# Local attention with queries and keys computed feature-down, their squared lengths taken through DRAM, and the condition set-up moved behind the experts

## The chip, the cores and the metric

The program runs on one core of a Trainium2 chip. The metric is the device time of one execution in microseconds; the time before is the median of three runs. The engines are TensorE (PE), VectorE (DVE), ScalarE (ACT), GpSimd (POOL) and SyncE (SP); the queue from which an instruction or a transfer is issued is named after its engine.

## The reference, cut to what matters

Four sequences of 512 tokens with 256 features pass five stages: a mixture of 8 experts (two per token), a linear attention with 8 heads, a softmax attention with 16 heads whose result is mixed with a "field" that depends on a condition vector per sequence, and two layers of a local attention with a gated feed-forward. Two places matter here.

The local attention of each layer normalises queries and keys, rotates them, and attends within a window:

```python
q = l2norm(q) * qs                 # per head: 8 heads of 64 features
k = l2norm(k) * ksc
q, k = rotary_xpos(q, k)           # t*cos*scale + rotate_half(t)*sin*scale
...
sim = jnp.einsum('bhwid,bhwjd->bhwij', bq, bk)
attn = jax.nn.softmax(sim, axis=-1)
```

The length that `l2norm` divides by belongs to a token and a head. Rotation mixes feature d with feature d+32 of the same head and keeps token and head.

The field is a small chain on the conditions alone, four rows for the four sequences:

```python
fp = _layernorm(jax.nn.relu(consciousness_state @ We1.T + be1) @ We2.T + be2, ln_g, ln_b)
fa = jax.nn.softmax(jnp.einsum('be,se->bs', fp, pe), axis=-1)
```

## The kernel before

The work is one stream of stages: routing and experts, linear attention, softmax attention with conditions, then the local layers. A framework puts waits between instructions and orders each engine's queue by its own model of times; where the program says `PE.in_order()`, PE's queue keeps the order in which the lines are written. All matrices are float32; a matmul leaves two records in the trace.

**Experts (from about L1480).** The chosen tokens of each expert are gathered (POOL's queue), pass three matrices, and are scattered to `ys` in DRAM (POOL's queue). 22 slots run always; two more (`rare`) stand in an `If` on a value read from the chip. The condition set-up `conditions` (L230 to L274: `csb`, `hdT`, a layer norm over four rows to `fp`, two small transposes, the product `pfs` with the position table, a softmax over 512 positions to `fa`, four transposes to `faT`) is called at the last of the 22 slots, ahead of its first layer. Then come three matmuls without use (`busy(3)`), the `If`, six more (`busy(6)`), and the seam: `results(0)` loads `ys` back as `g` (SP's and ACT's queues), `weighted` combines it to `ymoe` (L1530, L1531), and the linear attention starts with transposes of `ymoe`. What `conditions` makes is first used in the softmax attention.

**Local layers (`local_stream`, L563 to L880).** Each sequence ("batch") of a layer has a front, an attention in four steps c (two heads each), and a tail. Order in the loop `for k in range(4 * B + 1)`: scores of step c, first half; fill; values of step c-1; fill; scores of step c, second half; fill. The fill comes from `beside(b)`: the front of batch b+1, the tail of batch b-1, and for the last batch the feed-forward. `spend(n)` takes n pieces of it; before, 2 at each of the three places in batches 0 to 2, and 1 in batch 3. `run(fill)` takes what is left at the start of the next batch. Ahead of the loop, `lead` runs the whole front of batch 0 and two pieces of batch 1's front; for the second layer `lead` is woven with the rest of the first layer's feed-forward, one piece to one.

A front before (L590 to L649) has 22 pieces. It transposes the batch to `yT` (2 pieces), then per token tile and for queries and keys projects with tokens down (`pdq`: 128 tokens x 512 features), takes the squares on ACT (L614), sums them per head on DVE (`ss`, L615), multiplies by the tables from PSUM on DVE (L617, L621) and adds on POOL (`qr`, L624): 8 pieces. Lengths become reciprocals (L628 to L630). The values tiles `v` are 4 pieces. Then `qr` of the queries is scaled (L639) and both are transposed to features down, four transposes and one ACT copy at a time (`pqt`, L642 to L646), 8 pieces. The keys' reciprocal length goes in as the per-partition scale of the exponential (L666, two per tile since the scale differs by key tile). `qT`/`kT` share their memory slots (two each) with `uB`/`uA` of the feed-forward.

Denominators take a trip: `pz` is copied to `z`, written to DRAM (`sums`), read as 128 x 16 (`rden`), inverted, written (`rows`), read back spread over partitions (`zb`), and multiplied into `oT` (L698 to L708), all on SP's queue.

## Time and profile before

| | us |
|---|---|
| three runs | 1388.95, 1391.64, 1391.56 |
| median | 1391.56 |
| profiled execution | 1386.44 |
| its span (first to last instruction) | 1384.7 |
| PE busy in the span | 1335.9 |

| stretch of the span, us | what runs | PE busy, us |
|---|---|---|
| 0 to 310 | routing, experts | 81.7, 100.0, 99.8 in the first three hundreds |
| 310 to 335 | last expert, seam | see the lines that follow |
| 335 to 460 | linear attention | 46.3 of 400 to 450 |
| 460 to 720 | softmax attention | 38 to 49 of each 40 to 50 |
| 720 to 1385 | local layers | 50 of each 50 until 1350, 29.2 of the last 34.7 |

The profile gives for each group of equal instructions a line: line of the program, engine, operation, output<-inputs with partitions x elements, count, then busy time and mean duration in ns, then the engine's idle time just ahead of them and what ended it. In a timeline a line is: start, length, engine, line, operation, count, and in brackets the idle time before it with what released it. Where several instructions are merged the length reaches from the first start to the last end. Matmul records overlap their neighbours at the ends; what a group costs PE is read from its start to the next group's start.

### The profile page before, as it was taken

Reading aid. Unit: us, or ns where it says so; the run is one execution under the profiler, and the core shown is the slowest. Engines: PE = TensorE matmul, PEld = TensorE weight load, DVE = VectorE, ACT = ScalarE, POOL = GpSimd, SP = SyncE. Lnnn points to the kernel's source line nnn. Section 1 sums busy time; section 2 is a strip of 40 time slices with the busy share of each in tenths; the row PEclk is TensorE's granted clock in tenths of the full one; section 3 lists DMA queues with packets and bytes.
Section 4 is the critical chain, followed back from the end, with each engine's and each line's share of the span. In section 5 each row is a group of like instructions: output and inputs, shape, how many; then the busy total and the mean of one; then the engine's idle time right before and its main releaser. Section 6 shows DMA issues by size and latency. Waiting matters only on the chain.

```text
span 1384.7 us, 19465 instructions
## 1 busy us (share of the span) xinstructions
PE 1335.9 (96%) x7632; PEld 827.5 (60%) x7632; DVE 653.3 (47%) x1295; ACT 587.7 (42%) x997; POOL 232.8 (17%) x223
## 2 busy tenths in 40 slices
PE   5999999998999999999999999999999999999998
PEld 4788888874566633333334555656555566556654
DVE  6222212224777643332227687654362777854421
ACT  4111111125555355454655756662223667474111
POOL 1325322211000011010104232100020322310110
PEclk7999999999999999999999999999999999999999
DMA  4577667633000000000210001210001010011000
GB/s 143 209 261 271 226 218 250 208 121 126 1 1 1 1 1 1 1 1 1 88 53 21 17 25 32 78 40 24 23 1 42 24 33 25 17 40 41 22 24 25
DMA packets 43085, 94.74 MB, mean 68 GB/s; under 512 B 9568, under 2 KB 25064, under 8 KB 40168
## 3 DMA queue, kind: packets, MB, share of 16 engines
q1 hardware_dynamic: 37560, 81.81, 17.8%
q0 software_dynamic: 3792, 10.24, 2.2%
q10 hardware_dynamic: 1632, 1.34, 0.3%
q8 instruction: 63, 1.03, 0.3%
q14 instruction: 38, 0.31, 0.1%
HBM read 84.08 MB, written 7.21 MB: 66 GB/s over the span
## 4 chain that ended last, share of the span: by engine, by line
PE 89%; DVE 5%; ACT 2%; DMA 2%; issue 1%; SPq 0%; DVEq 0%; POOLq 0%; POOL 0%; ACTq 0%
PE ph L78 14%; PE pdq L78 12%; PE pfy L78 6%; PE pug L78 5%; PE pv L78 5%; PE pua L78 5%; PE sc L78 5%; PE po L78 4%; PE pn L78 4%; PE pdy L78 4%; PE pds L78 4%; PE pz L78 2%; PE pqt L82 2%; PE pqk L78 1%; PE pf L78 1%
## 5 line engine op out<-in xcount | busy, mean ns | idle before, releaser
L78 PE MATMUL pdq<-wqkv,yT 128*128 128x512 f32 x384 | 177.1, 602 | 0.0
L416 ACT ACTIVATE cex<-sc 128x1024 f32<-128x1024 f32 x128 | 124.0, 1021 | 96.7 <-PE sc L78 95.9
L78 PE MATMUL ph<-h,w 128*128 128x256 f32 (+1 forms) x704 | 133.4, 347 | 0.5 <-ACT h L1398 0.5
L624 POOL TENSOR_TENSOR qr<-t,t 128x512 f32<-128x512 f32 x64 | 85.9, 1343 | 266.4 <-DVE t L621 221.7
L668 DVE TENSOR_TENSOR p<-p,lmask 128x384 f32<-128x384 f32 (+1 forms) x128 | 92.4, 736 | 68.4 <-ACT p L666 67.2
L78 PEld LDWEIGHTS ph<-h,w 128*128 128x128 f32 x704 | 116.1, 191 | 12.9 <-ACT h L1398 0.7
L78 PEld LDWEIGHTS pdq<-wqkv,yT 128*128 128x128 f32 x384 | 69.6, 190 | 78.1 <-issue 72.8
L1398 ACT ACTIVATE h<-ph,w 128x256 f32<-128x256 f32 (+1 forms) x88 | 35.4, 438 | 182.7 <-PE ph L78 130.1
L1400 DVE TENSOR_SCALAR h<-ph,w 128x256 f32<-128x256 f32 (+1 forms) x88 | 36.1, 438 | 162.4 <-PE ph L78 109.2
L666 ACT ACTIVATE p<-pds,ss 128x256 f32<-128x256 f32 (+1 forms) x256 | 96.1, 457 | 39.1 <-PE pds L78 30.6
L78 PE MATMUL pug<-hT,w 128*128 128x512 f32 x160 | 76.8, 602 | 0.0
L78 PE MATMUL sc<-qm,kT 32*128 32x512 f32 x512 | 75.2, 639 | 0.2 <-ACT cex L416 0.2
L78 PE MATMUL pua<-hT,w 128*128 128x512 f32 x160 | 75.2, 592 | 0.0
L614 ACT ACTIVATE sq<-pdq 128x512 f32<-128x512 f32 x64 | 38.3, 598 | 85.2 <-PE pdq L78 49.2
L78 PE MATMUL pv<-cex,v 128*32 128x512 f32 x512 | 69.0, 604 | 2.1 <-DVE xT L290 2.1
L78 PE MATMUL ph<-xbT,w 128*128 128x256 f32 (+1 forms) x352 | 68.5, 347 | 0.5 <-ACT xbT L123 0.5
L387 POOL TENSOR_SCALAR fterm<-vw,faT 128x256 f32<-128x256 f32 x16 | 14.6, 925 | 320.3 <-DVE cr L377 320.3
L78 PE MATMUL po<-w,h 128*128 128x256 f32 x296 | 67.7, 380 | 0.5 <-ACT h L1398 0.5
L78 PE MATMUL pds<-qT,kT 64*128 64x256 f32 (+1 forms) x512 | 65.3, 375 | 0.0
L78 PEld LDWEIGHTS pds<-qT,kT 64*128 64x128 f32 x512 | 43.9, 186 | 32.9 <-issue 25.8
L78 PEld LDWEIGHTS ph<-xbT,w 128*128 128x128 f32 x352 | 58.4, 191 | 7.7 <-issue 0.9
L78 PE MATMUL pdy<-wo,oT 128*128 128x256 f32 x256 | 61.5, 386 | 0.0
(301 smaller groups left out, 2129.9 us busy)
## 6 DMA issues: line engine op xcount, KB each, us to landing
w<-in_moe_w_dram SPq DMA_DIRECT2D x22, 1024.0 KB, 6.3
w<-in_moe_w_dram SPq DMA_DIRECT2D x22, 640.0 KB
w<-in_moe_w_dram SPq DMA_DIRECT2D x22, 516.0 KB, 3.8
zb<-rows SPq DMA_DIRECT2D x32, 256.0 KB, 4.0
g<-ys SPq DMA_DIRECT2D x6, 512.0 KB, 5.1
wqkv<-in_f_wqkv_dram SPq DMA_DIRECT2D x2, 1536.0 KB
w<-in_f_w_dram SPq DMA_DIRECT2D x2, 1408.0 KB, 6.1
out_dram<-yc SPq DMA_DIRECT2D x16, 128.0 KB, 1.8
```

The costliest lines, as they stand in the source:

```text
L78: cls._queue(nc.tensor.matmul(*args, **kw))
L82: cls._queue(nc.tensor.transpose(*args, **kw))
L387: nc.gpsimd.tensor_scalar_mul(fterm[:, t, :], vw, W["faT"][:, t, b : b + 1])
L416: nc.scalar.activation(ex, pss[j], AF.Exp, scale=CHD**-0.5)
L614: nc.scalar.activation(sq, p3, AF.Square)
L624: nc.gpsimd.tensor_tensor(qr_t[:, s], t1, t2, ALU.add)
L666: nc.scalar.activation(p[:, at], pss[r][:, at], AF.Exp, scale=d.ss[:, 2 * u + jj, 1, 2 * c + r : 2 * c + r + 1])
L668: nc.vector.tensor_tensor(p[:, :n], p[:, :n], lmask[:, :n], ALU.mult)
L1398: nc.scalar.activation(dst, src, AF.Relu, bias=bias)
L1400: nc.vector.tensor_scalar(dst, src, bias, 0.0, ALU.add, ALU.max)
```

## The change

1. In the front, queries and keys are projected with features down (`piece`): the weight block is stationary, 512 tokens move. ACT copies the product into `qT`/`kT`; SP copies the partner features (32 partitions apart) to `sw`; ACT squares; DVE multiplies both by the tables (now laid out features down, with the learned scale as a per-partition scalar); POOL adds. No transposes follow.
2. The squares are summed over the 64 features of a head by matmuls with `heads32` (`lengths`); the 16 x 512 sums go to DRAM (ACT's queue), come back as 128 x 64 (POOL's queue), are inverted, go to DRAM again (POOL's queue), come back spread over partitions (`zb`, SP's queue, 8 transfers per front), and scale queries and keys on DVE. The exponential needs no scale and becomes one per tile.
3. A front has 14 pieces. `lead` takes all of the first and 8 of the second; `spend` follows a table; the tail of the batch before comes after 12 pieces. `tab` is loaded once, `b2` with the feed-forward's weights, `zb` has two buffers.
4. `conditions` becomes three parts: the first ahead of the `If`, the second ahead of the seam's last `busy`, the third a filler of the linear attention. Four of the nine matmuls without use go.

```diff
@@ conditions
         nc.vector.tensor_tensor(fp, fp, row("lnb")[:B, :], ALU.add)
+        yield
         pt = tpt("pfpT")
...
         mm(ps[:B, :], [(fpT[:, c, :], W["peT"][:, c, :]) for c in range(2)])
+        fa = cp.tile([B, S], F32, tag="fa", name="fa", bufs=1)
+        nc.vector.tensor_copy(fa, ps[:B, :])
+        yield
...
-        nc.vector.reduce_max(fmx, ps[:B, :], axis=AX.X, negate=True)
+        nc.vector.reduce_max(fmx, fa, axis=AX.X, negate=True)
...
-        nc.scalar.activation(fa, ps[:B, :], AF.Exp, bias=fmx, accum_out=fsum)
+        nc.scalar.activation(fa, fa, AF.Exp, bias=fmx, accum_out=fsum)
@@ local_stream
+        heads32 = dw.tile([128, 32], F32, tag="heads32", name="heads32")
+        nc.gpsimd.memset(heads32, 0.0)
+        for r in range(2):
+            nc.gpsimd.memset(heads32[64 * r : 64 * r + 64, 16 * r : 16 * r + 16], 1.0)
@@ front
+            def piece(s, c):
+                at = s * DIN + c * 128
                 ps = mmt("pdq")
+                mm(ps, [(w.wqkv[:, 0, at : at + 128], yT[:, 0, 1 : S + 1]), (w.wqkv[:, 1, at : at + 128], yT[:, 1, 0:S])])
+                dst = (d.qT, d.kT)[s]
+                nc.scalar.copy(dst[:, c, :], ps)
+                if c % 2 == 0:
+                    return
+                dst = dst[:, c - 1 : c + 1, :]
+                sw = lp.tile([128, 2, S], F32, tag="sw", name="sw", bufs=3)
+                for g in range(4):
+                    nc.sync.dma_start(sw[32 * g : 32 * g + 32], dst[32 * (g ^ 1) : 32 * (g ^ 1) + 32])
+                sqs[s, c // 2] = lp.tile([128, 2, S], F32, tag="sq", name="sq")
+                nc.scalar.activation(sqs[s, c // 2], dst, AF.Square)
+                for i, t in enumerate((sw, dst)):
+                    at = 4 * w.l + 2 * (1 - i) + s
+                    nc.vector.scalar_tensor_tensor(
+                        t, t, qks[:, at : at + 1], tab[:, 2 * s + 1 - i, :].unsqueeze(1).to_broadcast([128, 2, S]),
+                        ALU.mult, ALU.mult)
+                nc.gpsimd.tensor_tensor(dst, dst, sw, ALU.add)
+            def lengths(s):
+                ps = mmt("pl")
+                for c in range(4):
+                    PE.matmul(ps[32 * c : 32 * c + 32, :], heads32, sqs[s, c // 2][:, c % 2, :], start=True, stop=True)
+                z = lp.tile([128, S], F32, tag="z", name="z", bufs=1)
+                nc.scalar.copy(z, ps)
+                nc.scalar.dma_start(sums[s * DH : (s + 1) * DH], z[0:128:16, :])
+            for s in range(2):
+                for c in range(4):
+                    piece(s, c)
+                    if s and c == 1:
+                        lengths(0)
                     yield
...
             for t in range(NT):
...
+                if t == 1:
+                    lengths(1)
+                    rl = lp.tile([128, 2 * DH * S // 128], F32, tag="rl", name="rl", bufs=1)
+                    nc.gpsimd.dma_start(rl, sums.rearrange("h q -> (h q)").rearrange("(p n) -> p n", p=128))
+                    nc.scalar.activation(rl, rl, AF.Sqrt)
+                    nc.vector.tensor_scalar_max(rl, rl, 1e-12)
+                    nc.vector.reciprocal(rl, rl)
+                    rows_ = dr.tile([2 * DH, S], F32, tag="lrows", name="lrows")
+                    nc.gpsimd.dma_start(rows_.rearrange("h q -> (h q)").rearrange("(p n) -> p n", p=128), rl)
+                    for c in (0, 2):
+                        for s, dst in enumerate((d.qT, d.kT)):
+                            zb = lp.tile([128, 2, S], F32, tag="zb", name="zb")
+                            for r in range(2):
+                                nc.sync.dma_start(
+                                    zb[64 * r : 64 * r + 64],
+                                    rows_.rearrange("(s c r) q -> s r c q", r=2, s=2)[s, r, c : c + 2].partition_broadcast(64))
+                            nc.vector.tensor_tensor(dst[:, c : c + 2, :], dst[:, c : c + 2, :], zb, ALU.mult)
                 yield
@@ scores
-                for jj in range(2):
-                    at = slice(jj * 256, min(jj * 256 + 256, n))
-                    nc.scalar.activation(p[:, at], pss[r][:, at], AF.Exp,
-                                         scale=d.ss[:, 2 * u + jj, 1, 2 * c + r : 2 * c + r + 1])
+                nc.scalar.activation(p, pss[r][:, :n], AF.Exp)
@@ values
-            zb = lp.tile([128, 2, S], F32, tag="zb", name="zb", bufs=1)
+            zb = lp.tile([128, 2, S], F32, tag="zb", name="zb")
@@ first_two, beside, the loop
             def lead():
-                for _ in range(20):
-                    next(first)
-                    yield
-                for _ in range(2):
+                yield from first
+                for _ in range(8):
                     next(second)
                     yield
-                yield from first
...
-                    for _ in range(9 if b else 7):
+                    for _ in range(12 if b else 0):
...
+                more = ((2, 3, 2), (2, 2, 1), (1, 1, 1), (1, 1, 1))
+                share = (((1, 1, 1), (1, 0, 0)) + ((0, 0, 0),) * 2, more, more, ((1, 1, 1),) * 4, ((1, 1, 1),))
...
-                    spend(2 if b < B - 1 else 1)
+                    spend(share[b][c][0])
@@ experts, seam
             for j, d in enumerate(often):
-                if j == len(often) - 1:
-                    conditions(cw_, wp)
...
-            busy(3)
+            aside = conditions(cw_, wp)
+            next(aside)
+            busy(1)
             with tc.If(halves > NHALF - NRARE):
...
-            busy(6)
+            busy(3)
+            next(aside)
+            busy(1)
...
-                        fill = (beside(b) if b else chain(rest, beside(0))) if b < B else iter(())
+                        fill = (beside(b) if b else chain(rest, aside, beside(0))) if b < B else iter(())
```

The per-layer scaling of `tab` on DVE, `ss`, `qr` and the transposes of the old front go with it.

## The prediction

> **What bounds the kernel now.** I read the page's busy shares and 40 slices first, then the busy time by stretches, the groups by form, and the timeline at the three places that the change touches.
>
> ```profile
> PE 1335.9 (96%) x7632; PEld 827.5 (60%) x7632; DVE 653.3 (47%) x1295; ACT 587.7 (42%) x997; POOL 232.8 (17%) x223
> ...
> PE   5999999998999999999999999999999999999998
> ```
>
> The stretches (start:end, length, then PE, PEld, DVE, ACT, POOL), two of the local attention:
>
> ```profile
> 850.00:900.00 50.00, 50.00 (x319) 30.31 (x320) 38.26 (x75) 29.14 (x64) 11.08 (x10) 1.00 0.21 65
> ...
> 1150.00:1200.00 50.00, 49.85 (x306) 29.56 (x303) 42.43 (x83) 31.75 (x66) 16.11 (x11) 1.00 0.11 28
> ```
>
> TensorE (PE) works 50 of 50 us, DVE 38 to 42. From 750 to 1350 us PE never rests for as much as 0.5 us, so there a microsecond of PE work is a microsecond of time, and work of the others costs nothing unless PE must wait for it.
>
> **PE work in the local stage.** The projections of queries and keys stay 16 matmuls of 512 columns per front with weights and tokens changing sides (a pair holds PE 1.72 to 1.81 us either way): 0. What goes and what comes:
>
> ```profile
> L78 PE MATMUL pv<-cex,v 128*32 128x512 f32 x512 | 69.0, 604 | 2.1 <-DVE xT L290 2.1
> ...
> L82 PE MATMUL pqt<-ident,qr 128*128 128x128 f32 x256 | 33.9, 277 | 0.8 <-DVE qr L639 0.8
> ```
>
> The 256 transposes (32 in each of 8 fronts) go. Their 33.9 us hold tails that overlap the next group; start to start eight of them hold PE 1.02 us and sixteen 1.89, which is 3.9 to 4.1 us per front, 31.4 in all. `lengths` adds two groups of four 128x32 matmuls of 512 columns per front, 16 groups. `pv` has that very shape: four of them side by side, 64 groups in 69.0 us, 1.08 each; start to start 0.99. I take 16.4 (15.8 to 17.3). Net **-15.0 us**.
>
> DVE and ACT work is covered by PE. DVE per front: before 8 x (0.68 + 0.68 + 0.75) + 4 x 0.68 + 1 = 20.6 us; after 8 products and 4 scalings of 128x1024 at 1.22 (row of L1593) plus 0.8, 15.4. ACT loses half of its 256 exponentials (0.39 start to start). POOL keeps its sum: 4 adds of 128x1024 at 2.44 (row of L751) for 8 at 1.34. The 16 `sw` copies per front pass SP at 0.35 to 0.65 each, some 8 us of a 50 us batch, and are needed only after that front's lengths. If this cover were gone, DVE would have to pass 50 us per batch; it falls. The smaller loads (`tab` once, `qks`, `b2`) lie tens of us ahead of their use: 0.
>
> **The conditions.** In before they stand in front of the last expert.
>
> ```profile
> 304.55 0.28 PE L82 MATMUL pfpT<-ident,fp 4*128 4x4 f32 x2 [1.18 <-DVE fp L254]
> ...
> 305.09 1.88 PE L78 MATMUL pfs<-peT,fpT 128*4 128x512 f32 x4 [0.26 <-DVE fpT L259]
> ...
> 306.90 2.05 PE L78 MATMUL ph<-xbT,w 128*128 128x128 f32 x16
> ...
> 317.23 0.97 POOL L1466 DMA_INDIRECT ys<-ob,goal  x1 [9.14 <-DVE ob L1461]
> ```
>
> They hold PE from 297.40 to 299.65 (2.25 us), from 303.30 to 306.90 (3.60), and about 0.6 more around 309. Without them the last expert, the scatter (317.23) and everything behind come 6.4 us earlier. After, the same work lies in the gap between that scatter and the first `ymoe` (at 325.58; 8 us) and takes the place of four `pbusy`. Price there: the layer norm's ACT step (1.28 table load + 0.29) must end before ACT issues its half of the `g` loads behind the branch, 0 to 1.8 us; the table goes back for the features, 0 to 1.28. I take 1.4: **-5.0 us** (-6.4 to -3.3).
>
> **The added wait.** Lengths used to stay on chip (sqrt, reciprocal, scale, some 3 us). Now they go through DRAM twice, and the first scores of a batch wait for that. The nearest rows are the denominators' trip, on SP's queue:
>
> ```profile
> 782.67 0.63 SPq L698 DMA_DIRECT2D sums<-z  x1
> 784.43 0.34 SPq L699 DMA_DIRECT2D rden<-sums  x1
> 787.50 0.33 SPq L702 DMA_DIRECT2D rows<-rden  x1
> 788.92 1.31 SPq L705 DMA_DIRECT2D zb<-rows  x2
> ```
>
> and DVE's product at its end:
>
> ```profile
> 793.67 1.29 DVE L708 TENSOR_TENSOR oT<-oT,zb 128x512 f32<-128x512 f32 x2 [1.79 <-DMA zb<-rows]
> ```
>
> From the issue of `sums` to the product 11.0 us, hidden because its user comes a batch later. The new trip, from the last `lengths` matmul: ACT copy and issue 1.1; `sums` 1.75; `rl` on POOL's queue; table load, sqrt and semaphores 1.7; max and reciprocal 0.7; `rows` on POOL's queue; four `zb` instead of two 4.75 + 1.5; the second product of 128x1024, 1.2; to PE 0.2. A plain POOL transfer is not in the stage: at least SP's 1.4 to 1.6 us, at most the gather's 4.4; nearest is the last scatter on that queue, 2.96 with 0.97 of issue where a plain one issues in 0.6, so 2.6. Sum 18.1 (bounds 15.9 to 21.7). In-order queues add: the denominators' reciprocal came 1.2 to 2.2 us after its data (in the trip above at 787.23, landing 1.6 after 784.43), behind masks on DVE. One such delay per trip: **c = 19.3 us**. While ACT's sqrt or DVE's product waits, exponentials and masks queue behind it, and PE's `values` for them; these have 5 us of slack.
>
> What PE has to do between the second `lengths` and the scores that need it, by rows (v tile or piece 1.81, lengths 1.0, scores 1.06 + 0.85, values 1.67, pz 1.65, output tile 1.81):
> - Batch 0 of layer 0: two v tiles 3.6, transposes 1.0, six pieces 10.9, one lengths 1.0: 16.5 us. Waits 2.8.
> - Batch 1 of each layer: its second lengths comes in step 1 of batch 0, whose later steps have no filler: 2.5 + 5.2 + 3.6 + two v tiles 3.6 = 15.0. Waits 4.3, twice: 8.6.
> - Batches 2 and 3: steps 2 and 3 with output tiles and two v tiles, 19.7. Waits 0, four times.
> - Batch 0 of layer 1 has over 40 us of feed-forward beside it. But the second front takes its `qT`/`kT` slots early, in turn with `uB`/`uA` of batch 3's feed-forward, so its first copies wait for the last output matmul, and four copies and two squares (4.1 us + 0.6) stand against two pieces (3.6): 1.2.
>
> Together **+12.6 us**.
>
> [...] DVE's masks (two SBUF inputs) beside POOL's adds: at 800.64 two of 128x384 took 2.09 us, where two took 1.18 at 789.83 without an add. [...] No row here shows a plain POOL transfer in the stage.
>
> **Sum.** -15.0 - 5.0 + 12.6 = -7.4 us. The profiled execution took 1386.4 us (span 1384.7); the median of the three runs is 1391.6, 5.2 above it. -7.4 on the median gives **1384 us**.
>
> **Rivals.**
> - Everything hidden: c at or under 16, as with both POOL hops at SP's 1.5 us and no queue delay. Waits 1.2 to 3, the conditions free: -15.0 - 6.4 + 1.5 = -20, **1371**. For it: all bounds at their good end; against: DVE hops were late in each of the first four trips.
> - Slower, by the length trip at the start of each batch. All four places wait once c passes 19.7, and then each us of c costs 7. The waits eat the 20 us at c = 20.6; from there it is slower. With three delays like the reciprocal's, c = 22.5: 6.0 + 15.0 + 11.2 + 1.2 = 33.4, +13.4, **1405**. For it: the trip has six engine hops where the denominators' has two, the bound is 21.7 without delays. Against: while PE waits, the queues run dry and the hops are prompt.
> - No change: c from 20.2 to 21, waits of 17 to 23, **1391**.
> - The sums of squares don't run side by side: 64 matmuls at 0.86 instead of 16.4 us, +39 - 7 = +31, **1423**. The rows of `pv` and `pz` speak against it.
>
> **Chances.** Forecast (c 18 to 20.1) 0.40; all hidden 0.15; no change 0.13; slower by the trip 0.30; not side by side 0.02. A measurement of this kernel tells about 0.2% (2.8 us) from no change: faster 0.55, same 0.13, slower 0.32. The first two cases and the third reach from 1370 to 1394; the range must take in most of the slower case, to 1404, and leaves out some 0.2 at its ends.
>
> **What would show it.** `pqt` gone, a group of 128 records 128*32 128x512 of about 16.4 us in its place; PE's waits naming DVE's product with `zb` at the first `pds` of batches: about 3 us in layer 0's first, 4 in each second, near 0 at the third and fourth; the last scatter some 6 us earlier, the first `ymoe` 5. Wrong if waits at batches 2 and 3 exceed 1 us each, if PE idles inside steps (masks behind a blocked DVE), or if the seam gives under 3.

## The result and the profile after

The changed kernel takes 1399.57 us (median of 5 runs, 1398.10 to 1401.80) where before took 1391.56 on the same chip (5 runs, 1388.16 to 1391.70): a ratio of 1.0071, 95% interval 1.0058 to 1.0084. It is **slower**, by 8.0 us between the medians, where 7.4 us less was forecast. Its profiled execution has a span of 1397.8 us, against 1384.7.

The page after: the busy shares, and PE in 40 slices.

```profile
PE 1330.7 (95%) x7496; PEld 802.8 (57%) x7496; DVE 642.9 (46%) x1092; ACT 567.8 (41%) x852; POOL 237.8 (17%) x210
...
PE   5899999997999999999999899999999989999998
```

PE is busy for 5.2 us less, and the span is 13.1 longer: the time went into stops. The seam's slice fell from 8 to 7, and two in the local attention (769 to 804 and 1118 to 1153 us) from 9 to 8. (The second slice, in the experts, reads 8 for 9 too; the change doesn't touch them.) The stretches (columns as before) show that a full batch isn't where they are:

```profile
850.00:900.00 50.00, 50.00 (x295) 26.39 (x294) 38.00 (x61) 29.36 (x48) 13.26 (x8) 1.00 0.47 114
```

What PE waited for from 720 us on (total, times, longest). In before the longest row there was this:

```profile
PE pqt L82 <- DVE qr L639: 0.8, 1, 0.8
```

In the changed kernel the first rows are these:

```profile
PE pds L78 <- DVE kT L667: 6.3, 3, 3.3
PE pn L78 <- DVE p L686: 5.3, 4, 2.0
PE pdy L78 <- DVE oT L726: 1.9, 1, 1.9
```

The first row is the wait that was forecast (scores for lengths), at half its forecast size. The second wasn't forecast: `values` stands before masks. Both lie around batch 0 of each layer. From the first `pdt` of the local attention to the end, the kernel takes 673.6 us for 663.5: 10.2 of the 13.1. Another 1.7 are there already at the last full expert, before anything that changed (that point lies anywhere from 290.1 to 293.5 in these runs, whichever kernel), and 1.2 between.

**Batch 0 of layer 0**, from its first scores to those of batch 1. The stretch in before, then in the changed kernel:

```profile
748.90:788.00 39.10, 39.10 (x218) 21.07 (x216) 26.75 (x53) 27.54 (x58) 11.33 (x9) 1.00 0.01 1
```

```profile
763.60:797.30 33.70, 29.48 (x176) 14.87 (x177) 28.79 (x30) 19.32 (x32) 11.74 (x6) 0.95 0.48 119
```

PE's work in this stretch fell by a quarter (transposes gone, pieces moved ahead into the lead), DVE's didn't: 26.8 us beside 39.1 became 28.8 beside 29.5. Here DVE is as long as PE. PE and DVE inside it:

```profile
778.46 0.65 PE L78 MATMUL pn<-p,v 128*64 128x256 f32 x4
780.23 0.65 PE L78 MATMUL pn<-p,v 128*64 128x256 f32 x2 [1.12 <-DVE p L686]
782.84 1.99 PE L78 MATMUL pn<-p,v 128*64 128x256 f32 x10 [1.97 <-DVE p L686]
784.77 2.65 PE L78 MATMUL pz<-p,ones 128*32 128x256 f32 x32
```

```profile
773.39 3.92 DVE L686 TENSOR_TENSOR p<-p,lmask 128x384 f32<-128x384 f32 x3
777.24 1.27 DVE L625 SCALAR_TENSOR_TENSOR sw<-sw,qks,tab 128x1024 f32<-128x1024 f32 x1
778.43 1.27 DVE L625 SCALAR_TENSOR_TENSOR qT<-qT,qks,tab 128x1024 f32<-128x1024 f32 x1
779.63 3.76 DVE L686 TENSOR_TENSOR p<-p,lmask 128x384 f32<-128x384 f32 x3
```

One `values` takes from 778.46 to 784.83, 6.4 us where 1.73 is its length. It waits for masks that stand in DVE's queue behind two products of the second front, and that take 3.8 us by threes. The group of masks in batch 0, in before and in the changed kernel, and two of POOL's sums there:

```profile
L668 DVE TENSOR_TENSOR p<-p,lmask 128x512 f32<-128x512 f32 (+1 forms) x16 | 9.8, 619 | 15.6 <-ACT p L666 15.4
```

```profile
L686 DVE TENSOR_TENSOR p<-p,lmask 128x512 f32<-128x512 f32 (+1 forms) x16 | 14.3, 939 | 1.5 <-ACT p L685 1.5
```

```profile
773.61 2.55 POOL L628 TENSOR_TENSOR qT<-qT,sw 128x1024 f32<-128x1024 f32 x1 [15.86 <-DMA sw<-kT]
794.10 5.29 POOL L628 TENSOR_TENSOR kT<-kT,sw 128x1024 f32<-128x1024 f32 x1 [5.22 <-DVE kT L625]
```

A mask takes 939 ns on the mean there, for 619 in before. Either side can be the one that is stretched: the three masks from 773.39 took 3.92 us (1.76 in e8 below, without sums on POOL), and the sum beside them 2.55 (2.35 alone); the sum at 794.10 took 5.29, and the two masks beside it a usual 1.01. One reason why the products come so late is on SP's queue:

```profile
755.16 9.79 SPq L664 DMA_DIRECT2D zb<-lrows  x8
765.00 4.41 SPq L620 DMA_DIRECT2D sw<-qT  x7
769.54 9.11 SPq L620 DMA_DIRECT2D sw<-kT  x8
```

The eight loads of the first front's lengths wait for `lrows` and for free `zb` buffers, and the second front's swapped copies behind them get out only from 765 to 779.

**The clock.** After some of these stops the granted TensorE clock falls (the column behind POOL), once in the seam and twice here. After others it stays at 1.00: behind the 1.90 us before the first scores (763.6) and the 2.48 us in front of `pfpT` (320.3).

```profile
340.00:345.00 5.00, 5.00 (x12) 2.87 (x11) 2.89 (x4) 2.72 (x3) 0.00 (x0) 0.50 0.00 0
784.00:788.00 4.00, 4.00 (x43) 2.07 (x43) 2.52 (x4) 2.64 (x4) 2.04 (x2) 0.66 0.10 30
1130.00:1135.00 5.00, 4.36 (x22) 3.09 (x24) 1.16 (x2) 1.77 (x3) 0.00 (x0) 0.66 0.86 203
```

PE counts as busy there, so no row of waits shows this loss: `pz` above took 2.65 us for 1.72.

**The seam.** The last `ob` and the scatter come earlier, and PE's next work does not:

```profile
312.98 0.97 POOL L1488 DMA_INDIRECT ys<-ob,goal  x1 [2.31 <-DMA ys<-ob,goal]
...
320.30 0.25 PE L82 MATMUL pfpT<-ident,fp 4*128 4x4 f32 x2 [2.48 <-DVE fp L254]
...
320.91 1.88 PE L78 MATMUL pfs<-peT,fpT 128*4 128x512 f32 x4 [0.36 <-DVE fpT L260]
...
322.71 1.13 PE L78 MATMUL pbusy<-xres,ident 128*128 128x512 f32 x2
...
323.90 1.09 PE L82 MATMUL pt<-ident,ymoe 128*128 128x128 f32 x8
```

The scatter was at 317.23, the first `pt` at 324.65. Counted from the last full expert (`pxb`, 291.93 and 290.18) the scatter gains 6.0 us, `pt` (the first transposes of `ymoe`) 2.5, and the first `psc` (the linear attention's scores) nothing (53.2 us behind, 53.0 before).

### The profile page after: what moved, and what is told of

Same layout as the page of the kernel before. It is cut to its first block, busy times and chain, and to the rows that moved or that the text cites. A ratio compares the mean times of both kernels' runs of the same rounds, so it can differ in the third digit from the quotient of the medians.

```text
span 1397.8 us, 19169 instructions
## 1 busy us (share of the span) xinstructions
PE 1330.7 (95%) x7496; PEld 802.8 (57%) x7496; DVE 642.9 (46%) x1092; ACT 567.8 (41%) x852; POOL 237.8 (17%) x210
## 4 chain that ended last, share of the span: by engine, by line
PE 80%; DVE 10%; DMA 5%; ACT 3%; issue 2%; SPq 1%; ACTq 0%; DVEq 0%; POOL 0%; POOLq 0%
PE ph L78 14%; PE pdq L78 8%; PE pfy L78 6%; PE pv L78 5%; PE pug L78 5%; PE sc L78 5%; PE po L78 5%; PE pua L78 5%; PE pn L78 3%; PE pdy L78 3%; PE pdv L78 3%; DVE p L686 2%; PE pds L78 2%; PE pz L78 2%; DMA zb<-lrows 1%
## 5 line engine op out<-in xcount | busy, mean ns | idle before, releaser
L686 DVE TENSOR_TENSOR p<-p,lmask 128x384 f32<-128x384 f32 (+1 forms) x128 | 98.9, 804 | 47.9 <-ACT p L685 47.6
L78 PE MATMUL pdq<-yT,wqkv 128*128 128x512 f32 x256 | 119.4, 604 | 0.3 <-ACT yT L599 0.3
L685 ACT ACTIVATE p<-pds 128x384 f32<-128x384 f32 (+1 forms) x128 | 64.1, 544 | 43.8 <-PE pds L78 36.7
L78 PEld LDWEIGHTS pdq<-yT,wqkv 128*128 128x128 f32 x256 | 45.8, 189 | 55.1 <-issue 51.3
L628 POOL TENSOR_TENSOR qT<-qT,sw 128x1024 f32<-128x1024 f32 x16 | 40.6, 2539 | 198.1 <-DVE qT L625 123.5
L78 PE MATMUL pn<-p,v 128*64 128x256 f32 (+1 forms) x512 | 60.2, 364 | 5.3 <-DVE p L686 5.3
```

Source lines behind the costliest of these rows:

```text
L78: cls._queue(nc.tensor.matmul(*args, **kw))
L628: nc.gpsimd.tensor_tensor(dst, dst, sw, ALU.add)
L685: nc.scalar.activation(p, pss[r][:, :n], AF.Exp)
L686: nc.vector.tensor_tensor(p[:, :n], p[:, :n], lmask[:, :n], ALU.mult)
```

## The experiments

Each ratio is to runs of before on the same chip (its medians were 1388.6 to 1391.4), with its 95% interval; the changed kernel stands at 1.0071. Two theories to begin with: the **trip** (scores and DVE's queue wait for lengths) and **late masks** (DVE's products, locked against POOL's sums, hold the masks of batch 0). One caution holds for all of them: PE's order is written out, but the framework orders the other queues by its own estimates, so an edit also moves instructions in DVE's queue, and single microseconds between two kernels may be that (e1 below shows 2.7 us of it).

**1. The two halves (e1, e2).** e1 is the changed kernel with these lines of the seam as in before; e2 is before with them changed.

```diff
+   if j == len(often) - 1:
+       conditions(cw_, wp)
...
-   aside = conditions(cw_, wp)
-   next(aside)
-   busy(1)
+   busy(3)
...
-   busy(3)
-   next(aside)
-   busy(1)
+   busy(6)
```

> The changed kernel with the conditions put back in front of the last expert, as in before; the local attention stays changed. By the stretches of the two traces the local attention is 9.9 us longer (673.6 for 663.7) and the seam 1.4 us longer (432.0 for 430.6): then this kernel is 10 us over before, 1401.5, and 0.7216 of PE's seam comes back: the stretch from the start of the last experts to the local attention is within 1 us of before's 430.6. By my prediction's terms (-15.0 and +12.6 in the local attention, -5.0 in the seam) it would be 2.4 us under before, 1389.2.

> Before with the conditions alone moved into the seam. By the prediction's term it is 5.0 us faster than before (1386.6). By the traces of the two kernels the last scatter comes 7.7 us earlier against the start of the experts, but layer norm, transposes and POOL's sums then stand in front of the first transposes of the linear attention and PE's clock falls after the pause: the gain is given back, 0 to 1.5 us slower than before (1391.6 to 1393).

e1: 1401.46 us, 1.0093 (1.0079 to 1.0107). e2: 1388.37, 0.9993 (0.9984 to 1.0002). The loss is in the local attention, and the seam alone changes the time by -0.8 us (-2.2 to +0.3), not by -5.0. By e1 against the changed kernel (1.0093 to 1.0071) it would be some -3, but those intervals overlap. (The first text's "0.7216" is a slip; its claim is that e1 is within 1 us of before's 430.6 us up to the local attention. That missed: from `pxb` to the first `pdt` e1 takes 433.8 us and before 431.1, with the same lines of these stages.) In e2 `pt` came 2.5 us earlier against `pxb`, `psc` 0.5 later.

**2. Without the trip's wait (e3, e5, e9).** e3 and e5 leave queries and keys without their lengths, and give the exponential a scale of 0.001.

```diff
-   nc.vector.tensor_tensor(dst[:, c:c+2, :], dst[:, c:c+2, :], zb, ALU.mult)
+   nc.vector.tensor_tensor(zb, dst[:, c:c+2, :], zb, ALU.mult)              # e3
+   nc.vector.tensor_tensor(dst[:, c:c+2, :], dst[:, c:c+2, :], tab[:, 0:2, :], ALU.mult)   # e5
```

```diff
-   nc.scalar.copy(z, ps)
+   nc.scalar.activation(z, ps, AF.Ln)                  # e9
+   nc.scalar.activation(z, z, AF.Exp, scale=-0.5)
...
-   nc.gpsimd.dma_start(rl, sums.rearrange("h q -> (h q)").rearrange("(p n) -> p n", p=128))
...
-   nc.gpsimd.dma_start(rows_.rearrange("h q -> (h q)").rearrange("(p n) -> p n", p=128), rl)
+   rows_ = sums
```

> The changed kernel, but the products of lengths with queries and keys go to a tile that nobody reads (the output is of unscaled queries and keys, and the exponential has a scale of 0.001 so that it stays finite). Every transfer, every instruction of DVE, ACT, POOL and PE is still there; only the scores no longer wait for the lengths' trip. Theory of the trip (my prediction): its waits are 12.6 us, so this kernel takes 1387. Theory of the late masks: the trip's waits on PE in the trace are 6.3 us (three, on kT) and part of the rest is the mask products that come late in batch 0 because POOL's sums and DVE's products of the second front fall beside them; these stay, so it takes 1399.6 - 6.3 = 1393, and the waits of pn on p in batch 0 (5.3 us) are still in the trace.

> The changed kernel, but DVE's four scalings per front multiply by a constant tile of the same size in place of the lengths that come from DRAM (and the exponential has a scale of 0.001): the lengths aren't applied, but every instruction and transfer of the trip is still there. Neither PE nor DVE waits for the end of the trip any more. In the run where only the scores didn't wait, nothing was gained, since DVE stood at the same products for 28 us in all and masks and the layer norm behind them came late. Theory of the trip, with DVE's queue behind it: all stops of the local attention but those of before go, with the half clock after them: 1399 - 16 to 22 = 1377 to 1383. Theory of DVE's load in batch 0 (in the changed kernel DVE is busy without a gap from 769.8 to 787.1 with the second front's products and masks that POOL's sums stretch): the stops of batch 0 stay, and only the waits in front of batches go (1.9, 1.1, 3.3, and some 3 at the layer norm and the output tiles): 1390 to 1393.

> The changed kernel with a shorter trip: ACT makes 1/length out of the sums of squares at once (logarithm and exponential, with the factor -0.5; the lower bound of 1e-12 is left out), writes it to DRAM once, and the broadcast reads it from there. The load of rl, the square root, DVE's maximum and reciprocal and the write of lrows go: some 8 us of the trip's 18 (by the changed kernel's rows: from lsums issued at 746.0 to zb issued at 755.2 are 9.1 us, of which one landing of 1.8 stays). POOL's sums and DVE's products stay. Theory of the trip: its waits in front of batches (6.3 us) go, and so do DVE's stops at its products (32 us over the local attention) with what is late behind them (oT 1.9, hT 1.0) and the half clock after the waits (some 3): 1386 to 1389. Theory of the lock and DVE's load: the masks' stops in batch 0 (5.3 us and the half clock after) stay, and the gain is 6.3 plus 2 at most: 1391 to 1393. If the order that DVE's queue was given is what decides, it can go either way, as it did when the scores no longer waited.

e3: 1401.51, 1.0088 (1.0074 to 1.0101). e5: 1407.49, 1.0126 (1.0109 to 1.0142). e9: 1411.17, 1.0160 (1.0137 to 1.0184). The theory of the trip asked for 1377 to 1389 and got none of it. The waits moved: to masks (7.4 us in e3, 11.6 in e5, 10.5 in e9), in e3 to a layer norm (one wait of 5.7), and in e9, whose trip is shorter, to the lengths of later batches (10.7 us in six waits, the longest 5.4 in front of batch 1). In e9's batch 0 the first scores don't wait at all, and the masks do:

```profile
763.40 1.13 PE L78 MATMUL pds<-qT,kT 64*128 64x256 f32 x8
...
782.36 0.65 PE L78 MATMUL pn<-p,v 128*64 128x256 f32 x2 [3.48 <-DVE p L681]
```

So the trip isn't by itself what holds the time. That these three are even slower than the changed kernel I put down to DVE's order (in e5 scalings and products that need no wait stand ahead of more masks); that isn't shown by itself.

**3. Other places for pieces and copies (e4, e6, e7).**

```diff
-   share = (((1, 1, 1), (1, 0, 0)) + ((0, 0, 0),) * 2, more, ...
+   share = (((1, 1, 1),) + ((1, 0, 0),) * 3, more, ...        # e4
...
-   nc.sync.dma_start(sw[32 * g ...
+   nc.scalar.dma_start(sw[32 * g ...                          # e6
...
-   for _ in range(8): next(second); yield
+   yield from second                                          # e7, and no pieces in batch 0
```

> The changed kernel with another order of the pieces in batch 0: the second front's last two value tiles stand in steps 2 and 3 of batch 0, ahead of the products that wait for masks, and no longer behind the whole batch. The work and the trip are the same, and PE has as much to do between the lengths and batch 1. Theory of the late masks: batch 0 stops because no piece stands between the scores and the products there; a piece of 1.8 us in front of each of two products in each layer takes up to 4.6 us of stops and with them up to two stretches at half clock (1.9 and 1.6 us): 1393 to 1397. Theory of the trip: nothing changes, since the lengths' wait in front of batch 1 only grows by what the stops lose: 1399 to 1400.

> The changed kernel with the swapped copies issued on ACT's queue in place of SP's, where those of the second front stand behind the first trip's last loads (ready at 754, issued from 765 to 778.6). Theory of DVE's load in batch 0: the second front's products come some 8 us earlier, in the lead, where DVE has room (7.7 of 20 us busy); masks come on time: stops of 4.6 us in each layer and the half clock after them (1.9 and 1.6) shrink to half or less: 1391 to 1395. SP's queue also has no stop between the denominators' transfers: 1 to 2 us at the last output tiles. ACT issues 16 copies more per front at 0.5 us (8 us of 50, where it is busy for 28): 0. Theory of the trip: the products aren't its bound; the time stays at 1399.

> The changed kernel with the whole second front in the lead, in both layers: six pieces (11 us of PE and one group of lengths) go from batch 0 to the place in front of it. Theory of the trip: batch 0 and batch 1 are both covered (batch 0 by 11 us more, batch 1 by all of batch 0, 21 us): its waits of 1.9, 1.1 and 3.3 go and the stops at masks stay: 1393. Theory of DVE's load: the second front's products leave batch 0 for the most part (SP still holds their copies back by some 10 us), so the stops at masks shrink as well, though nothing is left to fill batch 0 while exponentials and masks are made (5.2 us of PE a step against some 4 of ACT and 3 of DVE): 1388 to 1394.

e4: 1405.58, 1.0120 (1.0105 to 1.0135). e6: 1445.81, 1.0402 (1.0388 to 1.0415). e7: 1416.97, 1.0191 (1.0178 to 1.0205). All my expectations missed. e4's pieces take PE ahead, and the wait comes back in front of batch 1 (lengths 10.3 us in six waits, the longest 4.7), while masks still cost 5.7. In e7, with no piece beside batch 0, `pn` waits 14.9 us and the scores of batch 1 once 9.0. Both fit an engine behind PE that is short of time. Neither shows it, since in both PE also comes earlier to what it waits for. e6 tells nothing of the queue, because ACT's is worse: four issues take it 2.45 us, and its squares stand behind them.

```profile
745.01 2.45 ACTq L620 DMA_DIRECT2D sw<-kT  x4
747.51 1.06 ACT L622 ACTIVATE sq<-kT 128x1024 f32<-128x1024 f32 x1 [1.97 <-DMA sw<-kT]
```

PE waited 16.2 us for these squares.

**4. The lock (e8, e10).** The sum on DVE, with the long trip and with e9's short one.

```diff
-   nc.gpsimd.tensor_tensor(dst, dst, sw, ALU.add)
+   nc.vector.tensor_tensor(dst, dst, sw, ALU.add)
```

> The changed kernel with the sum of the two products on DVE in place of POOL: four sums of 128x1024 more per front on DVE (an estimated 1.2 us each by the scaling's row of 1.22: 4.9 us per 50 us), and none on POOL. If masks are stretched by POOL's sums (three took 3.92 us at 773.39 and 3.76 at 779.63, where three took 1.63 to 1.76 at other places), DVE loses 2.1 us of stretch at two to three places in batch 0 and pays 4.9: the stops stay about as they are, 1397 to 1401, and in the batches with 38 us of DVE in 50 it has still room. If DVE's load in batch 0 isn't the matter but the lock is, stops of 4 us in each layer go: 1391 to 1393.

> The short trip and the sum on DVE together. The sum on DVE took all waits for masks away (5.3 us; the time fell by 4.3 of 1399) and left 8.8 us of waits for lengths in three places, with the half clock after each. If lock and trip are the two causes and nothing else, both go: from 1395 less 8.8 and some 4 of half clock: 1381 to 1385, faster than before (1389 to 1391). If DVE is simply too full in batch 0 (busy from 768 to 792 there), its waits come back at the masks: 1390 or more.

e8: 1395.40, 1.0040 (1.0028 to 1.0052): 4.3 us better than the changed kernel, though DVE has 4.9 us more per front. The waits for masks are gone, the masks of batch 0 take their usual time, and lengths are left:

```profile
L686 DVE TENSOR_TENSOR p<-p,lmask 128x512 f32<-128x512 f32 (+1 forms) x16 | 9.3, 620 | 0.2 <-ACT p L685 0.2
```

```profile
PE pds L78 <- DVE kT L667: 8.8, 3, 3.2
```

So the lock (a mask or a sum takes longer beside the other: 3.92 us for 1.76, and 5.29 for 2.35, in the rows above) is real, and taking it away is worth some 4 us net of DVE's longer work. It is also what made these masks late, and not DVE's amount alone: DVE is busy for 28.3 us of batch 0's 33.0 here, and no mask is late. e10: 1396.34, 1.0055 (1.0033 to 1.0077). Half the trip's length on top gives nothing; its waits are 4.5 us for lengths and again 5.4 for masks, with no sum on POOL, so the lock isn't the only thing that can make masks late.

**5. A queue of their own for the copies (e13, e14, e17).** The sum on DVE in all three; e14 and e17 have the short trip of e9 too.

```diff
-   nc.sync.dma_start(sw[32 * g ...
+   nc.gpsimd.dma_start(sw[32 * g ...            # e13, e14, e17
...
-   for _ in range(8):
+   for _ in range(6):                           # e17, in the lead
...
-   share = (((1, 1, 1), (1, 0, 0)) + ((0, 0, 0),) * 2, more, ...
+   share = (((1, 1, 1),) * 2 + ((1, 0, 0),) * 2, more, ...    # e17
```

> The kernel with the sum on DVE, and the swapped copies issued on POOL's queue, which has little else there then (loads and stores of rl, 0.6 us each), in place of SP's. In the kernel with the sum on DVE alone SP issued the second front's copies at 763.2 to 775.7, behind lengths' loads that waited from 753.9 to 763.1; its products then ran from 769 to 791 among the masks, and DVE was busy from 768 to 792. If the queue is the cause, the second front's first products come by 765, DVE's stretch in batch 0 loosens, the lengths of the second front reach batch 1 earlier (wait 3.0 to under 1 in both layers, with the half clock after them): 1395.4 less 4 to 8: 1387 to 1391. If DVE's amount of work in batch 0 is the cause whatever the order, or POOL's own waits hold the copies as SP's did, it is 1394 to 1397.

> Sum on DVE, short trip (1/length by logarithm and exponential on ACT, one pass through DRAM, the lower bound left out) and swapped copies on POOL's queue, which issues nothing else in the stage then. With lock, trip and queue all out of the way only DVE's and ACT's work in batch 0 is left. If these three are the causes: no wait over 1 us on PE in the local attention but those of before, 1378 to 1384, faster than before. If the placing of the second front's work in DVE's queue is the cause, masks in batch 0 still wait some 5 us with the half clock after them: 1388 to 1394.

> As the kernel with sum on DVE, short trip and the copies on POOL's queue, but six pieces of the second front in the lead in place of eight, and eight pieces among the four steps of batch 0 in place of four (two more behind the step's scores, and the last two value tiles in steps 2 and 3). PE's work in batch 0 grows by some 3.6 + 3.6 us, DVE's stays. Theory of DVE's load in batch 0: masks no longer wait (8.3 us in all there), the half clock after them goes, and the first scores still don't wait, since the short trip ends 6 us before them: 1394.2 less 6 to 10: 1384 to 1388, faster than before. If DVE's place in the queue decides and not its load, masks wait as long as there: 1393 to 1396.

e13: 1416.55, 1.0204 (1.0190 to 1.0218). e14: 1394.17, 1.0035 (1.0022 to 1.0047). e17: 1399.19, 1.0062 (1.0048 to 1.0076). In e13 the copies do come early, DVE takes a product of the second front ahead of the first front's scaling, stands at its copy for 5.1 us, and the first scores wait 12.4. In e14 no scores wait, with trip, lock and queue all out of the way, and PE's largest waits are for DVE's masks:

```profile
PE pn L78 <- DVE p L681: 8.3, 8, 1.8
```

Of these 4.7 us are in the two batches 0 (in layer 0's DVE is busy for 26.8 of 32.0 us), the rest in later batches. In e17, layer 0 does what the theory of load asks (from the first `pdt` to the first `pug`, the feed-forward's first product, 181.0 us for 183.1 in e14, masks of batch 0 wait 1.8), but in layer 1 PE waits 3.8 us for one mask, and the stages from the last expert to the local layers, which the edit doesn't touch, are 3 us longer. So it stays undecided whether the amount of DVE's work or its order makes the masks late.

**6. Half of the swap's work away (e18).**

```diff
-   for i, t in enumerate((sw, dst)):
+   for i, t in ((1, dst),):
...
-   nc.gpsimd.tensor_tensor(dst, dst, sw, ALU.add)
```

> The changed kernel without the product of the swapped copies and without the sum (queries and keys are multiplied by the first table alone, so the rotation is left out). The swapped copies are still transferred, lengths and their trip stay, PE's work is the same. DVE has 5.1 us less per front, POOL 9.8, and there is no lock by sums. Theory of DVE's load and the lock in batch 0: masks don't wait (5.3 us in the changed kernel), the maximum, the reciprocal and the scalings of the second front are prompt, so the waits in front of batch 1 (1.1 and 3.3) go too; only the lead's 1.9 to 2.5 and a little clock remain: 1387 to 1390. Theory of the trip: waits for lengths stay or grow, since PE comes earlier: 6 to 9 us in front of batches, 1394 to 1396, as with the sum on DVE.

e18: 1385.65, **0.9963** (0.9949 to 0.9977). PE's work, copies, lengths and trip are those of the changed kernel, and it is 1.08%, 15 us, faster than that, and 5 faster than before (expected: 1387 to 1390). Batch 0, and PE's waits from 720 us on:

```profile
765.10:795.00 29.90, 27.82 (x178) 14.41 (x178) 19.11 (x26) 19.00 (x32) 1.19 (x3) 1.00 0.55 138
```

```profile
PE pds L78 <- DVE kT L666: 4.7, 3, 1.9
...
PE pn L78 <- DVE p L685: 0.4, 1, 0.4
```

DVE is busy 19.1 us beside 27.8 of PE, and the stops at masks (all but 0.4 us) and the low clock are gone. The local attention takes 659.5 us, 14.1 less than in the changed kernel. The trip, untouched, waits 4.7 us.

SP issues the second front's copies as late as in the changed kernel (766.5 to 779.6 us, there 765.0 to 778.7), so their late place alone doesn't make the stops. e18 takes the lock and half of the products away at once, and e8 parts the two: it has no lock either, and does on DVE what e18 leaves out. By their ratios (1.0040 and 0.9963) e18 is 10.7 us faster than e8 (some 8 to 13). So of the 15 us some 4 come with the lock, net of e8's longer DVE work, and some 11 with DVE's own product and sum. Leaving these out also shortens the chain ahead of each scaling, and that isn't told apart from DVE's load.

**7. The clock (e11, e15, e16) and another seam (e12).** e11 and e15 put six or three useless matmuls of 512 columns into e8 in front of scores that wait; e16 puts one in front of each of two feature products of e2; e12 is e2 with the second part of the conditions in the linear attention.

```diff
+   if c == 0 and (b == 1 or l + b == 0):        # e11: 6, e15: 3
...
+       for _ in range(3): PE.matmul(ps, ident, tab[:, 0, :], start=True, stop=True)
...
+   if d is ds[0] and u == 1:                    # e16, in features
...
+       PE.matmul(ps, ident, xres[0].rearrange("p t h -> p (t h)")[:, :512], start=True, stop=True)
...
-   busy(3); next(aside); busy(1)                # e12
+   busy(5)
```

> The kernel with the sum on DVE, and six useless matmuls of 512 columns (some 2.7 us) in front of the scores that wait for lengths, in three places (waits of 2.5, 3.0 and 3.2 us). Nothing else of the work differs. After these waits the granted clock is 0.74, 0.66 and 0.74 over 5 us, and products that take 1.73 take 2.92. If it is the pause that lowers the clock, these stretches go back to full speed and some 1.3 us are won at each place: 1395.4 less 4 = 1391.5. If the clock falls for another reason, or the useless matmuls stand in the way of the scores, it is 1395 to 1397.

> As the kernel with useless matmuls in three places, but three of them instead of six: six took 5.3 us, where the waits were 2.5 to 3.2, and so stood in the way for 7.5 us in all, while the time rose by only 6 and the granted clock stayed at 1.00. Three take 2.7 us and fill the pauses. If the clock falls because of the pause, 1395.4 less 1.5 to 3: 1392.5 to 1394. If a pause that is filled costs as much as one that isn't, 1395.

> The kernel that changes the seam alone, with a useless matmul (0.9 us) in front of each of the two feature products that wait there (0.5 and 1.2 us), after which the granted clock is 0.50 from 340 to 345 and the values' projection takes 3.78 where it takes 1.99. If this clock eats the seam's gain, 1388.4 less 2: 1386.5, outside the interval of before. If the pauses before them (2.5, 1.1 and 1.0 us from 316 to 327) lower it, nothing changes: 1388 to 1389.5.

> Before with the conditions moved, as in the kernel that changes the seam alone (0.8 us under before, interval -2.2 to +0.3), but only their first part (layer norm) in the seam; the transposes, the product with the positions, its copy and maximum come as fillers in the linear attention. In the seam-only kernel the first transposes stood behind these, the copy of yT behind POOL's lock and the maximum, and a pause lowered the clock. If that ate the gain of 6.4, this gives 3 to 5 us: 1384.5 to 1386.5. If the last scatter and the loads behind it set the end in any case, it stays within 1 us of before, 1388 to 1390.

e11: 1401.40, 1.0082 (1.0067 to 1.0098); I had taken a matmul's price at half, and six stood in the way for 5.3 us. e15: 1392.35, **1.0024** (1.0015 to 1.0033), 2.2 us better than e8 (the intervals just overlap) for filling its pauses with nothing: the granted clock is 1.00 in every 5 us from 755 to 805. So the low clock comes with the pause, and costs about that. e16: 1392.03, 1.0020 (1.0009 to 1.0031). The clock is repaired, first e2, then e16:

```profile
340.00:345.00 5.00, 5.00 (x14) 3.61 (x13) 2.24 (x2) 2.59 (x3) 0.00 (x0) 0.50 0.00 0
```

```profile
340.00:345.00 5.00, 5.00 (x37) 4.19 (x36) 3.25 (x5) 1.62 (x3) 0.00 (x0) 1.00 0.00 0
```

`psc` comes 50.7 us behind `pxb`, 2.9 earlier than in e2, and 2.3 earlier than in before. Then linear and softmax attention take 6.7 us longer than in e2 from there to the local layers, with one wait of 3.8 for DVE's `aT` and a clock of 0.90 from 450 to 500; why isn't shown. e12: 1399.94, 1.0060 (1.0039 to 1.0081), expected 1384.5 to 1386.5, with seven runs from 1393.0 to 1401.6; the local layers begin 9 us later against `psc` than in e2, with `pfaT` waiting 4.6 us for DVE's `fa`: the work that left the seam was paid for in the linear attention.

No version that computes the whole came out measurably faster than before; e2 is level with it, and the best with the changed local attention, e15, is 3 us behind.

## Why the prediction was wrong

| step of the sum | forecast | measured |
|---|---|---|
| transposes out, `lengths` in | -15.0 | -1.94 per undisturbed batch (52.48 to 50.54 us from `pdt` to `pdt`, batch 1 of both layers, before and e18): -15.5 if all eight gain that. Right |
| conditions | -5.0 | -0.8 (e2; -2.2 to +0.3). Too good by 4 |
| waits for the trip | +12.6 | 6.3 in the changed kernel, 4.7 in e18. Too dear by half |
| DVE's and POOL's work | 0 | some +15 for half of the products and all sums (changed kernel against e18), of which 10.7 are DVE's (e8 against e18). **The step that failed** |

- **The failed step** is "DVE and ACT work is covered by PE ... If this cover were gone, DVE would have to pass 50 us per batch; it falls." The sum of DVE's work fell, and a full batch is indeed 50 us (its rows above show 50.00 of 50.00). But batch 0 isn't a full batch: the change itself takes transposes out of it and six more pieces of the second front (eight in the lead for two), and leaves 28 us of PE (27.8 in e18), while the second front's products, scalings and sums stay and come late. The cover had to be counted for this stretch: DVE 28.8 against PE 28. I did notice that its "later steps have no filler", and used it for the trip only. DVE's amount doesn't settle the form that the loss takes: in e8, with 28.3 us of DVE, no mask is late, and PE waits 8.8 us for lengths instead.
- "The 16 `sw` copies ... are needed only after that front's lengths": true of PE's need, but on SP they stand behind loads that wait, and their delay carries the products into batch 0. That these positions matter is in the rows; the attempts to give the copies another queue (e6, e13) brought other waits, and e18 has the same delay with next to no stop at masks, so its price by itself stays open.
- "These have 5 us of slack" (masks): they had none. PE waited 5.3 us for them.
- **The lock** was left out of the sum, though its rows in before were there (two masks took 2.09 us beside an add, 1.18 without). It struck the masks of batch 0: 939 ns for 619, worth 4.3 us (e8); three masks lost 2.2 us beside a sum of 2.55.
- **The trip** was mis-sized at its waits, not its length: from the last `lengths` matmul of the first front (745.3) to the scores (763.6) are 18.3 us, forecast 18.1 without delays. The lead waited 1.9 (forecast 2.8), batch 1 of the two layers 1.1 and 3.3 (4.3 each), batches 2 and 3 nothing (0). In front of layer 1's batch 0 the scores didn't wait, and a `lengths` took 2.05 us for 1.06 (forecast 1.2). A POOL hop, from the issue of a transfer on POOL's queue to the next engine's start, took 1.75 to 2.2 us in 15 of the changed kernel's 16 (3.0 once, with a copy ahead on ACT), not the 2.6 estimated from a scatter.
- **The seam**: the price of 1.4 counted ACT's table and left out PE's own order, by which `pfpT`, `pfs` and a `pbusy` stand ahead of `pt`, DVE's `yT` copy behind a maximum and a product that took 2.04 us for 0.47 beside POOL's sum, and the low clock (e16 against e2: 2.9 us at `psc`).
- **The clock** wasn't in the sum at all. In the changed kernel `pz` and `pn` after the stop took 2.65 for 1.72 us.
- The rival "slower by the trip" had the right sign and nearly the time (1405), but not the mechanism: it priced 33 us of waits for lengths, and there are 6. The conditions that I named as breaking the forecast, PE idling inside steps for masks and a seam under 3, are what happened.

The table's terms add to about +3 (with the trip's 4.7, since the +15 is counted from e18); the measured difference is 8.0 by the medians and 9.9 by the ratio. Of the rest, 2.8 us lie in batch 0's products even in e18 (2.14 and 2.51 us for 1.73, in both layers, and one wait of 0.4); 2 to 4 us I haven't placed.

## What to carry to other kernels

Count the cover of hidden work in the stretch where it will lie, after the change has taken its own PE work out of there, and not by an average batch. Where PE's order is fixed and what stands behind a late instruction in another queue is late too (SP's copies got out at 765.0, behind loads that held its queue for 9.8 us), taking a wait away moved it to the next late instruction (e3, e5, e9); taking away work of the engine that is full made the stops go (e18). That it can instead be put where PE has more to do isn't shown: e17 tried it and stayed undecided. Price a stop of PE with the clock that it may get back after it (0.50 after some stops here, with `pz` at 2.65 us for 1.72).

## What the runs showed of the hardware

- After some pauses of PE, of 1.5 to 3.3 us in all within 5 us, the granted clock was 0.50 for 2 to 6 us (in the changed kernel from 340 to 346, from 784 to 786 and from 1132 to 1134). Other pauses of 1.9 and 2.5 us left it at 1.00 (763.6 and 320.3), so their length alone doesn't tell. With useless matmuls in the pause it was 1.00 (e11, e15, e16): in e2 two waits of 0.5 and 1.2 us stand before a clock of 0.50 from 340 to 345, and with just these two filled it was 1.00 there (e16).
- A sum of 128x1024 on POOL (2.35 us alone) and DVE's masks and products beside it stretched one another. In the changed kernel three masks took 3.92 us (1.76 in e8) while the sum took 2.55, and a sum took 5.29 beside masks of the usual length. In its first lead both sides were stretched: a product of 128x1024 took 3.37 us for 1.28 (at 739.28) and the sum beside it 3.32 (at 738.25).
- DMA issues held up what stood behind them in an engine's queue: on SP the changed kernel's eight loads, which wait for data and buffers, for 9.8 us, with the second front's copies behind them, and on ACT four for 2.45 us of plain issuing (e6), with a square behind them.
